# Load stage of a diagonal-LSTM and quantum-layer kernel: small loads on another queue, the first image in other pieces, early matmuls and an early table load

## The chip, the cores and the metric

The kernel runs on one core of one Trainium2 chip. A core has a matrix engine (TensorE, PE in the profile), a vector engine (DVE), a scalar engine for activations (ACT), a general one (POOL, GpSimd), a queue engine (SP), and 16 DMA engines that move data between device memory and the core's on-chip memory. Each engine works through its own list of instructions in order and waits on semaphores for the others. DMAs are issued from the lists of SP, ACT and POOL.

The metric is the device time of one execution in microseconds (us). Several executions are timed; the median counts.

## The reference

The input is `x` of shape 16 x 128 x 64 x 64 (images, channels, rows, columns), fp32. There are two layers, each with a residual sum. `gn` is a group normalisation with 32 groups of 4 channels.

```python
def lstm(x, w_is, b_is, w_ss, b_ss):          # x: [16, 128, 64, 64]
    xs = skew(x)                              # row i shifted right by i: 127 columns
    i_s = einsum('oi,bihw->bohw', w_is, xs) + b_is
    def step(carry, ist):                     # one column of the skewed image
        h, c = carry                          # [16, 128, 64 rows]
        h_shift = h moved down by one row
        gates = ist + w_ss[:, :, 0] @ h_shift + w_ss[:, :, 1] @ h + b_ss
        o, f, i = sigmoid(gates[:, :384]) in three parts
        g = tanh(gates[:, 384:])
        c = f * c + i * g
        h = o * tanh(c)
        return (h, c), h
    return unskew(scan(step, zeros, columns of i_s))

x = x + lstm(gn(x), w_is, b_is, w_ss, b_ss)
xq = tokens(gn(x)) @ pre_w.T + pre_b          # 4 angles for each pixel
z = simulate(xq, q_weights)                   # 4-qubit circuit, 2 layers of rotations and CNOTs
x = x + image(z @ post_w.T + post_b)
```

`q_weights` (2 x 4 x 3) are the angles of the rotations; the kernel turns them into sines and cosines once.

## The kernel before

Channels lie on the 128 partitions. Forty of an image's 64 rows stay in on-chip memory, in the tile `ring` (16 images x 40 rows x 64 columns for each channel); the other 24 rows are read for their statistics only, through one of two buffers (`rest`, `trio`), and read again later. The program has three stages: the load stage, the scan of 160 diagonal steps (two bands of 32 rows share the partitions' columns), and the output stage. All stages are written out by hand (`manual_schedule`): each engine runs its instructions in the order in which the program emits them.

The change lies in the load stage (the block `with ExitStack() as prep`). Two things go on there side by side.

*Images and statistics.* SP issues, image by image, `rows(b)` (L258 to L265: the 40 rows for `ring`) and `behind(b)` (L269 to L274: the other 24). DVE runs `statistics(b, k)` (L295) on the eight chunks of 8 rows of each image. Chunk `k` is counted by place in `ring`: chunk 0 holds rows 32 to 39, chunk 1 rows 0 to 7, chunk 2 rows 8 to 15, chunks 3 and 4 rows 16 to 31; chunks 5 to 7 are in `rest` or `trio`. A buffer is refilled when DVE has done its three chunks. The last four images end with `aggregated(b)` on DVE (L300); POOL does the others (`gathering`).

*Inverse steps.* Pixels that no image reaches yet have a zero input, so their state is the same for all; the kernel computes it once as 33 steps on one column (`inv_step`, L194). A step is four matmuls of 128 x 128 on PE (each fp32 matmul runs as two passes), four gate activations on ACT with one product on POOL between, then three more activations on ACT, the last of which writes `hinv` for the next step. From the fourth step on two matmuls without use (`keep`, L183) follow on PE. They write one PSUM buffer (`ps_keep`, one buffer), of which nothing is read.

Before the first step stand, on each engine in this order:

- ACT: six DMA issues (two halves of `w_ss` into `ws_n`, `q_weights` into `qw`, `b_is` and `b_ss` into `b_n`, `w_is` into `wx_n`), the sine of `turned()` (L351), the copy of `wsT` from PSUM (L369), the copy of the biases (L374), then the gates.
- POOL: the identity matrix `ident` (`make_identity`), six small DMA issues (L286 to L291), the memsets of `hinv` and `cinv`, `turned()` (L342 to L350, from `qw` to the argument of the sine), the sum of the biases (L375).
- DVE: two statistics of image 0, two sums of the two taps of `w_ss` (L405, one for each half), then statistics.
- PE: four transposes into `wsT_ps` with `ident` (L368), one of the biases (L373), then the step's matmuls (L203).

Between the first steps stand the list `between`: the transposes of `w_is` (`wxT`), of the two taps of `w_ss` (`w0T`, `w1T`), and so on. `qw`, `wx_n` and `ws_n` are parts of the tiles named `spare` in the profile.

After the last step POOL copies `hinv` into the first state (L469, L470), PE starts the first scan step's matmuls (L481), in the middle of which it takes the group means of the statistics (L491). From these come mean and inverse deviation of each image, the first normalised diagonal on POOL, and the scan.

ACT needs the right function table in place: a table load (`ACT_TABLE_LOAD`) stands ahead of the first activation of another set.

Of the kernel before, what the change touches and what calls it, by code (L numbers as in the profile page):

```python
# [11 lines left out]
F32 = mybir.dt.float32  # L12
AF = mybir.ActivationFunctionType
# [3 lines left out]
P = 128  # L17
# [3 lines left out]
SLOTS = 32  # L21
# [13 lines left out]
AHEAD = RING - SLOTS  # L35
# [47 lines left out]
def kernel(  # L83
# [16 lines left out]
    nc = tc.nc  # L100
# [38 lines left out]
    def place(r):  # L139

        return (r + AHEAD if r < SLOTS else r - SLOTS) * NW

    def block(r):

        return ring[:, :, place(r) : place(r) + BLOCK]
# [18 lines left out]
    with ExitStack() as scan:  # L164
# [4 lines left out]
        wsT = wpool.tile([P, 512], F32, name="wsT")  # L169
# [3 lines left out]
        cinv = wpool.tile([P, NH], F32, name="cinv")  # L173
# [6 lines left out]
        stats = spool.tile([P, NB, NG2, 6], F32, name="stats")  # L180
        ps_small = scan.enter_context(tc.tile_pool(name="ps_small", bufs=1, space=PSUM))

        def keep(pool, tag, v):  # L183

            ps = pool.tile([P, v.shape[-1]], F32, name=nc.get_next_instruction_name(), tag=tag)
            nc.tensor.matmul(ps, lhsT=wsT[:, 0:P], rhs=v, start=True, stop=True)

        def fill(n):

# [43 lines left out]
        with ExitStack() as prep:  # L233
            pp = prep.enter_context(tc.tile_pool(name="prep", bufs=1))
# [3 lines left out]
            ps_keep = prep_ps.enter_context(tc.tile_pool(name="ps_keep", bufs=1, space=PSUM))  # L238
            prep.enter_context(tc.manual_schedule())

            sum_n, wx_n = (v.rearrange("p (g c) -> p g c", g=4) for v in spare[4:6])
            ws_n = [v.rearrange("p (g c) -> p g c", g=2) for v in spare[6:8]]
            b_n = pp.tile([8, P], F32, name="b_n", tag="rows")
            four_sb, prew, preb = (spare[3][0:4, a:b] for a, b in ((0, 272), (272, 400), (400, 401)))
            post_n, qw = spare[3][:, 404:408], spare[3][:, 408:432]
            ident = pp.tile([P, P], F32, name="ident")
# [10 lines left out]
            rests = {}  # L257

            def rows(b):
                half = SLOTS // 2  # L260
                for r, n in ((0, half), (half, half), (SLOTS, AHEAD)) if b < 2 else ((0, SLOTS), (SLOTS, AHEAD)):
                    nc.sync.dma_start(
                        out=ring[:, b, place(r) : place(r) + n * NW],
                        in_=xv[b, :, r * NW : (r + n) * NW],
                    )  # L265
# [3 lines left out]
            def behind(b):  # L269
                rest = both_rests[b % 2]  # L270
                rests[b] = [rest[:, i] for i in range(3)]
                of = xv[b, :, RING * NW :].rearrange("p (k n) -> p k n", n=CHUNK)
                for k in ((0, 1), (1, 2), (2, 3)) if b in (0, NB - 1) else ((0, 3),):
                    nc.sync.dma_start(out=rest[:, slice(*k)], in_=of[:, slice(*k)])  # L274

            ws_v = w_ss.rearrange("(g o) c k -> o g (c k)", o=P)
            for i in range(2):
                nc.scalar.dma_start(out=ws_n[i], in_=ws_v[:, 2 * i : 2 * i + 2])
            nc.scalar.dma_start(
                out=qw, in_=q_weights.rearrange("l w a -> (l w a)").partition_broadcast(P)  # L280
            )
            nc.scalar.dma_start(out=b_n[0:4], in_=b_is.rearrange("(g o) -> g o", o=P))
            nc.scalar.dma_start(out=b_n[4:8], in_=b_ss.rearrange("(g o) -> g o", o=P))
            nc.scalar.dma_start(out=wx_n, in_=w_is.rearrange("(g o) c -> o g c", o=P))
            make_identity(nc, ident)
            nc.gpsimd.dma_start(out=wide_sb, in_=wide)  # L286
            nc.gpsimd.dma_start(out=four_sb, in_=four)
# [7 lines left out]
            def statistics(b, k):  # L295
                v = ring[:, b, k * CHUNK : (k + 1) * CHUNK] if k < 5 else rests[b][k - 5]
                nc.vector.bn_stats(stats[:, b, k, :], v)
# [43 lines left out]
            def turned():  # L341
                nc.gpsimd.tensor_add(ang[:, 1, 0, :], q3[:, 0, :], q3[:, 2, :])  # L342
                nc.gpsimd.tensor_sub(ang[:, 1, 1, :], q3[:, 0, :], q3[:, 2, :])
                nc.gpsimd.tensor_copy(ang[:, 1, 2, :], q3[:, 1, :])
                nc.gpsimd.tensor_scalar(
                    ang[:, 0], ang[:, 1], 1.0 / (4.0 * math.pi), 0.25, ALU.mult, ALU.add
                )
                nc.gpsimd.tensor_scalar_mul(ang[:, 1], ang[:, 1], 1.0 / (4.0 * math.pi))
                nc.gpsimd.tensor_scalar(rnd, ang, ROUND, ROUND, ALU.add, ALU.subtract)
                nc.gpsimd.tensor_sub(ang, ang, rnd)  # L350
                nc.scalar.activation(trig, ang, AF.Sin, scale=TWO_PI)  # L351
# [13 lines left out]
            def transposed(name, to, of):  # L365
                tp = ps_prep.tile([P, 512], F32, name=f"{name}_ps", tag="tp")
                for g in range(4):
                    nc.tensor.transpose(tp[:, g * 128 : (g + 1) * 128], of(g), ident)  # L368
                nc.scalar.copy(to, tp)  # L369

            def biases():
                tp = ps_prep.tile([P, 8], F32, name="bias_ps", tag="tp")
                nc.tensor.transpose(tp, b_n, ident[0:8, 0:8])  # L373
                nc.scalar.copy(bias8, tp)  # L374
                nc.gpsimd.tensor_add(bias, bias8[:, 0:4], bias8[:, 4:8])  # L375
# [12 lines left out]
            def output_weights():  # L388
# [6 lines left out]
                nc.scalar.copy(w_out, tp)  # L395

            rows(0)
            rows(1)
            behind(0)
            turned()  # L400
            for k in (1, 2):
                statistics(0, k)
            for i in range(2):
                v = ws_n[i]
                nc.vector.tensor_add(sum_n[:, 2 * i : 2 * i + 2], v[:, :, 0::2], v[:, :, 1::2])  # L405
            transposed("wsT", wsT, lambda g: sum_n[:, g, :])
            biases()

            def cleared():
                for v in (*hst, *xns, none, cst[:, :, 0:LEAST]):  # L410
                    nc.gpsimd.memset(v, 0.0)
                    yield
                nc.gpsimd.memset(eps, EPS)
                nc.gpsimd.tensor_sub(apart_of, ident, group)
                yield
                nc.gpsimd.memset(w_image, 0.0)
                yield
# [21 lines left out]
            for b in range(NB):  # L439
                while b < NB - 1 and done * (NB - 1) < EARLY * (b + 1):  # L440
                    inv_step(done, ps_inv)
                    some()
                    if done > 2:
                        for _ in range(2):
                            keep(ps_keep, "keep", wsT[:, 0:P])
                    if between:
                        between.pop(0)()
                    done += 1
                if b + 2 < NB:
                    rows(b + 2)  # L450
                if b + 1 < NB:
                    behind(b + 1)
                    for k in ORDERED:
                        statistics(b + 1, k)
                for k in (5, 6, 7):
                    statistics(b, k)
                if b >= 3 * GATHER:
                    aggregated(b)
                if b and b <= 3 * GATHER and b % GATHER == 0:
                    behind_pool.append(gathering(b - GATHER))  # L460
# [15 lines left out]
            ps = ps_small.tile([P, 2, NB], F32, name="gm1", tag="small")  # L476
            var = pp.tile([P, NB], F32, name="var1")
            for g in ORDER:
                first[g] = ps_gate.tile([P, 2, NC], F32, name=f"ps0_{g}", tag="gate")
                for w, rhs in ((w1T, hst[0][:, :, 0 : LEAST // 2]), (w0T, above(hst[0], 0, LEAST // 2))):  # L480
                    nc.tensor.matmul(  # L481
                        first[g][:, :, 0 : LEAST // 2],
                        lhsT=w[:, g * 128 : (g + 1) * 128],
                        rhs=rhs,
                        start=w is w1T,
                        stop=True,
# [8 lines left out]
            ps = ps_gate.tile([P, NB], F32, name="gv1", tag="gate")  # L495
# [167 lines left out]
        def gate_ps(t):  # L663

            a, b = wide(t, LEAST // 2)
            ps = {} if t else first
            for g in ORDER:
                if t:
                    ps[g] = ps_gate.tile([P, 2, NC], F32, name=f"ps{t}_{g}", tag="gate")
                nc.tensor.matmul(  # L670
                    ps[g][:, :, a:b],
                    lhsT=wxT[:, g * 128 : (g + 1) * 128],
                    rhs=xns[t % 2][:, :, a:b],
                    start=t > 0,
                    stop=True,
                    skip_group_check=True,
                )
            if twice(t):
                nc.tensor.matmul(
                    ps[GO][:, 1, a:b],  # L680
                    lhsT=wxT[:, GO * 128 : (GO + 1) * 128],
                    rhs=xns[t % 2][:, 0, a:b],
                    start=False,
                    stop=True,
                    skip_group_check=True,
                )
            return ps
# [275 lines left out]
        with tc.manual_schedule():  # L963
            normalised(0)
            normalised(1)
            ps = gate_ps(0)
            for t in range(NSTEP):
                ps = step(t, ps)
# [7 lines left out]
            warm = small.tile([P, 1], F32, name="warm", tag="inv_t")  # L976
            nc.scalar.activation(warm, shift, AF.Sqrt)
            ps = ps_small.tile([P, 2, NB], F32, name="gm3", tag="small")
# [11 lines left out]
            v = block(NH - ROWS).rearrange("p i (r w) -> p i r w", w=NW)[:, :, :, NW - STRIP :]  # L990
# [30 lines left out]
            ps = ps_small.tile([P, NB], F32, name="mr_ps", tag="small")  # L1021
# [221 lines left out]
```

## Time and profile before

| | us |
|---|---|
| median of 3 runs | 1403.12 (1402.34 to 1403.14) |
| the profiled execution | 1402.86 |
| its span | 1401.1 |
| PE busy | 1348.3 |
| DVE busy | 975.5 |
| POOL busy | 885.4 |
| ACT busy | 786.5 |

The span is the time from the first instruction to the last of the profiled execution; the rest of its time lies around it. Busy time is the union of an engine's instructions. The times of instructions below count from the start of the span.

The page divides the span into 40 slices of 35 us. Each digit is the busy share in tenths, the last row the rate of the DMA engines:

```
PE   6788999999999999999999999999999999989995
DVE  6973565577767776677776777766666566876996
DMA  9950000000000000133333100000000000004999
GB/s 359 418 210 1 2 1 1 1 1 1 1 1 1 0 1 1 61 121 121 120 121 120 61 1 1 1 1 1 1 1 1 1 0 1 2 30 145 388 402 357
```

The load stage is the first 95 us or so: the DMA engines are busy, DVE nearly so, PE less. Then comes the scan, in which PE is busy.

### The profile page before, as it was taken

To read this page: it belongs to the slowest core of one execution; us is meant where nothing else is said; L and a number is where in the kernel's file an instruction comes from. 1 tells how busy PE (TensorE), PEld (TensorE's weight loads), DVE (VectorE), ACT (ScalarE), POOL (GpSimd) and SP (SyncE) were. 2 spreads that over 40 slices of the span, in tenths; PEclk is the share of its full clock that TensorE was granted. 3 is DMA by queue.
4 is the path that set the end of the run, shared out by engine and by line. 5 is a ranking of instruction groups with operands and counts; after the bars stand their busy time and mean duration, and the time that the engine had idled before them with its cause. 6 is when DMAs were issued, how large, how long until landed. Compare 5 with 4: busy or idle time off the path is not lost.

```text
span 1401.1 us, 19953 instructions
## 1 busy us (share of the span) xinstructions
PE 1348.3 (96%) x6028; PEld 964.8 (69%) x6028; DVE 975.5 (70%) x2526; ACT 786.5 (56%) x1880; POOL 885.4 (63%) x1578
## 2 busy tenths in 40 slices
PE   6788999999999999999999999999999999989995
PEld 4668888777767777777777667776777778886332
DVE  6973565577767776677777776666665566876996
ACT  5765666555555555555555555555555566654331
POOL 3236777776666777777777766777777667653300
PEclk9999999999999999999999999999999999999998
DMA  9950000000000000133333100000000000004999
GB/s 359 418 210 1 2 1 1 1 1 1 1 1 1 0 1 1 61 121 121 120 121 120 61 1 1 1 1 1 1 1 1 1 0 1 2 30 145 388 402 357
DMA packets 58027, 107.03 MB, mean 76 GB/s; under 512 B 4368, under 2 KB 32048, under 8 KB 56128
## 3 DMA queue, kind: packets, MB, share of 16 engines
q1 hardware_dynamic: 53280, 94.39, 18.4%
q0 software_dynamic: 3408, 10.58, 2.1%
q8 instruction: 48, 0.79, 0.2%
q10 hardware_dynamic: 1232, 0.80, 0.2%
q14 instruction: 59, 0.48, 0.1%
HBM read 59.61 MB, written 46.14 MB: 75 GB/s over the span
## 4 chain that ended last, share of the span: by engine, by line
PE 84%; DVE 3%; ACT 1%; issue 1%; POOL 1%; DVEq 0%; ACTq 0%; POOLq 0%
PE ps L849 47%; PE ps L670 30%; PE po_None L1125 3%; PE theta_None L1074 2%; PE am_None L1103 1%; DVE spare L934 1%; DVE stats L798 0%; DVE ps L924 0%; PE po L1125 0%; DVE cst L927 0%; DVE ring L1143 0%; ACT g L868 0%; DVE ps L864 0%; ACT g L928 0%; ACT ps L868 0%
## 5 line engine op out<-in xcount | busy, mean ns | idle before, releaser
L670 PE MATMUL ps<-spare,wxT 128*128 128x512 f32 (+18 forms) x1280 | 479.7, 518 | 0.6 <-POOL spare L661 0.6
L864 DVE TENSOR_TENSOR ps<-ps,both 128x256 f32<-128x256 f32 (+9 forms) x536 | 219.7, 410 | 294.4 <-PE ps L849 291.2
L868 ACT ACTIVATE ps<-ps,bias 128x512 f32<-128x512 f32 (+23 forms) x480 | 279.5, 583 | 218.5 <-DVE ps L864 182.1
L670 PEld LDWEIGHTS ps<-spare,wxT 128*128 128x128 f32 x1280 | 231.0, 190 | 173.1 <-issue 155.4
L849 PE MATMUL ps<-trio,w1T 128*128 128x256 f32 (+14 forms) x1088 | 306.4, 363 | 0.0
L849 PE MATMUL ps<-trio,w0T 128*128 128x256 f32 (+14 forms) x1088 | 305.6, 362 | 0.0
L899 ACT COPY both<-ps 128x256 f32<-128x256 f32 (+9 forms) x536 | 189.6, 356 | 181.0 <-PE ps L849 161.4
L849 PEld LDWEIGHTS ps<-spare,wsT 128*128 128x128 f32 x1088 | 196.1, 190 | 78.3 <-DVE spare L934 30.6
L849 PE MATMUL ps<-spare,wsT 128*128 128x256 f32 (+14 forms) x1088 | 243.4, 365 | 1.8 <-DVE spare L934 1.6
L707 POOL TENSOR_TENSOR ring<-ring,spare 128x256 f32<-128x256 f32 (+15 forms) x375 | 231.5, 644 | 17.9 <-DVE spare L934 17.9
L849 PEld LDWEIGHTS ps<-trio,w1T 128*128 128x128 f32 x1088 | 201.7, 190 | 22.2
L849 PEld LDWEIGHTS ps<-trio,w0T 128*128 128x128 f32 x1088 | 201.2, 190 | 21.1
L661 POOL TENSOR_TENSOR spare<-spare,rstd 128x512 f32<-128x512 f32 (+10 forms) x160 | 170.9, 1068 | 14.2 <-DVE rstd L505 1.7
L655 POOL TENSOR_TENSOR spare<-ring 128x256 f32<-128x256 f32 (+13 forms) x165 | 139.4, 845 | 0.0
L928 ACT ACTIVATE g<-cst 128x256 f32<-128x256 f32 (+20 forms) x320 | 102.9, 368 | 63.7 <-DVE cst L927 63.3
L934 DVE TENSOR_TENSOR spare<-g,ps 128x256 f32<-128x256 f32 (+17 forms) x319 | 105.4, 368 | 44.4 <-ACT g L928 39.7
L697 POOL TENSOR_TENSOR trio<-spare 128x240 f32<-128x240 f32 (+9 forms) x136 | 102.7, 755 | 37.3 <-DVE spare L934 33.8
L649 POOL TENSOR_TENSOR spare<-ring,mean 128x256 f32<-128x256 f32 (+15 forms) x191 | 122.6, 642 | 2.5 <-DVE mean L494 2.0
L868 ACT ACTIVATE g<-ps,bias 128x512 f32<-128x512 f32 (+20 forms) x160 | 97.3, 608 | 27.8 <-DVE ps L864 21.9
L927 DVE TENSOR_TENSOR cst<-cst,ps 128x256 f32<-128x256 f32 (+20 forms) x320 | 104.5, 368 | 5.5
L924 DVE TENSOR_TENSOR ps<-ps,g 128x512 f32<-128x512 f32 (+20 forms) x160 | 94.9, 593 | 18.2 <-ACT g L868 18.1
L916 DVE TENSOR_TENSOR cst<-cst,ps 128x512 f32<-128x512 f32 (+20 forms) x160 | 92.7, 580 | 16.8 <-POOL spare L231 9.6
(379 smaller groups left out, 1161.7 us busy)
## 6 DMA issues: line engine op xcount, KB each, us to landing
out_dram<-ring SPq DMA_DIRECT2D x93, 256.0 KB, 4.9
ring<-in_x_dram SPq DMA_DIRECT2D x14, 1024.0 KB, 9.7
low<-ring SPq DMA_DIRECT2D x6, 2048.0 KB, 7.6
ring<-in_x_dram SPq DMA_DIRECT2D x6, 2048.0 KB, 8.2
trio<-in_x_dram SPq DMA_DIRECT2D x7, 768.0 KB, 7.6
rest<-in_x_dram SPq DMA_DIRECT2D x7, 768.0 KB, 7.9
ring<-low POOLq DMA_DIRECT2D x18, 256.0 KB, 6.8
ring<-in_x_dram SPq DMA_DIRECT2D x16, 256.0 KB, 9.9
```

The lines of the kernel that those rows point to most:

```text
L649: op = nc.gpsimd.tensor_sub(by_pairs(xn, 0, j0, j1), x0, over(mean1, j1 - j0))
L655: op = nc.gpsimd.tensor_sub(by_pairs(xn, 1, j0, j1), lower, of)
L661: nc.gpsimd.tensor_mul(v, v, r)
L670: nc.tensor.matmul(ps[g][:, :, a:b], lhsT=wxT[:, g * 128 : (g + 1) * 128], rhs=xns[t % 2][:, :, a:b], start=t > 0, stop=True, skip_group_c ...
L707: op = engine.tensor_add(x1, x1, by_pairs(new, q, j0, j1))
L849: nc.tensor.matmul(out, lhsT=w[:, g * 128 : (g + 1) * 128], rhs=rhs, start=False, stop=True, skip_group_check=True,)
L864: nc.vector.tensor_add(v, v, both[g][:, a:b])
L868: nc.scalar.activation(to[:, :, a:w], ps[g][:, :, a:w], FUNC[g], bias=bias[:, g : g + 1])
L899: nc.scalar.copy(both[g][:, a:b], ps[g][:, 0, a:b])
L927: nc.vector.tensor_add(c[:, q], c[:, q], ig[:, q])
L928: nc.scalar.activation(th[:, q, a:w], c[:, q], AF.Tanh)
L934: nc.vector.tensor_mul(new[:, q, a:v], th[:, q, a:v], act[GO][:, q, a:v])
```

## The change

In words:

- `q_weights`, `b_is` and `b_ss` are issued from POOL, ahead of `make_identity`, and no more from ACT.
- `w_is` is issued from SP, between the rows of image 0 and of image 1.
- Image 0's rows come as 8, 24 and 8 (before: 16, 16 and 8), and image 1's as 32 and 8 (before: 16, 16 and 8).
- `keep` takes its weights as an argument; twelve of them with `ident` as weights and as data stand ahead of the transposes of `wsT`.
- DVE's first instructions change order: statistic of chunk 1, sum of the first half of `w_ss`, statistic of chunk 2, sum of the second half.
- After the biases an activation of one column with Sigmoid is added, whose result is not used.

```diff
-        def keep(pool, tag, v):
+        def keep(pool, tag, v, w=wsT[:, 0:P]):
             ps = pool.tile([P, v.shape[-1]], F32, name=nc.get_next_instruction_name(), tag=tag)
-            nc.tensor.matmul(ps, lhsT=wsT[:, 0:P], rhs=v, start=True, stop=True)
+            nc.tensor.matmul(ps, lhsT=w, rhs=v, start=True, stop=True)
...
             def rows(b):
-                half = SLOTS // 2
-                for r, n in ((0, half), (half, half), (SLOTS, AHEAD)) if b < 2 else ((0, SLOTS), (SLOTS, AHEAD)):
+                for r, n in ((0, AHEAD), (AHEAD, SLOTS - AHEAD), (SLOTS, AHEAD))[b > 0 :]:
+                    if b and r < SLOTS:
+                        r, n = 0, SLOTS
                     nc.sync.dma_start(
...
             for i in range(2):
                 nc.scalar.dma_start(out=ws_n[i], in_=ws_v[:, 2 * i : 2 * i + 2])
-            nc.scalar.dma_start(
+            nc.gpsimd.dma_start(
                 out=qw, in_=q_weights.rearrange("l w a -> (l w a)").partition_broadcast(P)
             )
-            nc.scalar.dma_start(out=b_n[0:4], in_=b_is.rearrange("(g o) -> g o", o=P))
-            nc.scalar.dma_start(out=b_n[4:8], in_=b_ss.rearrange("(g o) -> g o", o=P))
-            nc.scalar.dma_start(out=wx_n, in_=w_is.rearrange("(g o) c -> o g c", o=P))
+            nc.gpsimd.dma_start(out=b_n[0:4], in_=b_is.rearrange("(g o) -> g o", o=P))
+            nc.gpsimd.dma_start(out=b_n[4:8], in_=b_ss.rearrange("(g o) -> g o", o=P))
             make_identity(nc, ident)
...
             rows(0)
+            nc.sync.dma_start(out=wx_n, in_=w_is.rearrange("(g o) c -> o g c", o=P))
             rows(1)
             behind(0)
+            for _ in range(12):
+                keep(ps_keep, "keep", ident, ident)
             turned()
-            for k in (1, 2):
-                statistics(0, k)
             for i in range(2):
                 v = ws_n[i]
+                statistics(0, 1 + i)
                 nc.vector.tensor_add(sum_n[:, 2 * i : 2 * i + 2], v[:, :, 0::2], v[:, :, 1::2])
             transposed("wsT", wsT, lambda g: sum_n[:, g, :])
             biases()
+            warm = pp.tile([P, 1], F32, name="warm1")
+            nc.scalar.activation(warm, cinv[:, 0:1], AF.Sigmoid)
```

## The prediction

> **What bounds the kernel now.** I read the page first (shares, chain of waits), then the timeline of the load stage's two ends, then SP's waits, then the windows of one microsecond.
>
> ```profile
> span 1401.1 us, 19953 instructions
> PE 84%; DVE 3%; ACT 1%; issue 1%; POOL 1%; DVEq 0%; ACTq 0%; POOLq 0%
> ```
>
> TensorE's scan holds the span; the change doesn't touch it. Whatever is won or lost must come from the time at which the scan can start. The timeline around that start (start, length, engine, line):
>
> ```profile
> 92.52 0.29 ACT L210 ACTIVATE hinv<-inv_t,inv_a 128x1 f32<-128x1 f32 x1
> 92.61 0.37 DVE L300 BATCH_NORM_AGGREGATE mv<-stats 128x2 f32<-128x48 f32 x1
> 93.00 0.18 POOL L470 COPY spare<-hinv 128x1 f32<-128x1 f32 x1
> 93.24 0.49 PE L481 MATMUL ps<-spare,w1T 128*128 128x128 f32 x2 [0.78 <-POOL spare L470]
> 94.23 0.29 PE L491 MATMUL gm<-mv,w_amp 128*128 128x16 f32 x2
> ```
>
> Two chains arrive almost together. The 33 inverse steps end with `hinv` at 92.81 and release POOL L470, then PE L481. The statistics end at 92.98 (L300); the mean's matmul L491 needs them, yet waits for L481's matmuls until 94.23. So the steps bound, and the statistics stand 94.23 - 93.08 = 1.15 us behind (0.1 us for the hand-over). How the steps begin:
>
> ```profile
> 8.68 0.20 POOL L342 TENSOR_TENSOR w_image<-spare 128x8 f32<-128x8 f32 x1 [3.73 <-DMA spare<-in_L_conv_q_weights_dram]
> 10.71 0.24 ACT L351 ACTIVATE w_image<-w_image 128x48 f32<-128x48 f32 x1 [5.50 <-POOL w_image L350]
> 10.86 0.57 ACT L369 COPY wsT<-wsT_ps 128x512 f32<-128x512 f32 x1
> 12.42 1.28 ACT L210 ACT_TABLE_LOAD   x1 [0.93 <-PE inv_ps L203]
> 13.72 0.72 ACT L210 ACTIVATE inv_a<-inv_ps,bias 128x1 f32<-128x1 f32 x4
> 15.38 2.07 PE L203 MATMUL inv_ps<-hinv,wsT 128*128 128x128 f32 x8 [0.91 <-ACT hinv L210]
> 21.90 1.16 PE L203 MATMUL inv_ps<-hinv,wsT 128*128 128x128 f32 x8 [0.62 <-ACT hinv L210]
> ```
>
> The transposes of `wsT` were done at 9.1, but their copy stood behind the Sin, which waits for `qw`. The same eight passes take 2.07 us at first and 1.16 from 21.90 on: `hinv` ends at 15.32, 18.58, 21.84, 24.18, so steps 1 and 2 take 3.26 us and later ones 2.34.
>
> **The change, part by part.** *Small loads to POOL.* `make_identity` now stands behind three issues. POOL's issues last 0.71 (`wide_sb`, 128 partitions) and 0.50 to 0.55 us, so `ident`, done at 1.29 before, is done at 1.29 + 0.71 + 2 x 0.54 = 3.1 (2.8 to 3.4, three of 0.50 or three of 0.71). [...]
>
> [...]
>
> *Twelve fillers.* They need only `ident` and stand on PE ahead of the transposes. A filler is L186's shape; each waits for the one before it, having one PSUM buffer:
>
> ```profile
> 22.89 0.38 PE L186 MATMUL I-294_295<-wsT 128*128 128x128 f32 x2
> 23.34 0.49 PE L186 MATMUL I-297_298<-wsT 128*128 128x128 f32 x2
> L203 PE MATMUL inv_ps<-hinv,wsT x24: 420/421/582, 11.6 to 20.3; 128*128 128x128 f32 x24
> ```
>
> The second one shows the price with its wait: 0.49 + 0.07 of gap = 0.56 us at full rate. At the early rate a pass takes 421 ns against 273, so a filler takes 0.56 + 2 x 0.15 = 0.86. When does the rate rise? PE worked 11.57 to 14.47, paused, then worked nearly unbroken from 15.38 to 20.6, where it rose; so 2.9 us weren't enough and 5.2 were. Fillers keep PE 0.79/0.86 = 92% busy from 3.1 on, so I put the rise at 6.0 to 8.3, middle 7.15. That is 4.7 fillers at 0.86 and 7.3 at 0.56: they end at 7.15 + 7.3 x 0.56 = 11.2 (10.8 to 11.7). That is later than `wsT`'s data (second half landed at 7.93, added by 8.4; all that is ahead of it now, 1.8 MB, is what had moved by 8 us before) and later than the Sin: the fillers set the start. Four transposes at full rate take 0.7 (half of 1.16, plus the tail), so the copy starts at 11.9 instead of 10.86.
>
> [...]
>
> *Sigmoid table.* Before, copy to first gate took 13.72 - 10.86 = 2.86, since the load waited 0.93 us for PE. Now it follows the bias copy (ended 0.64 after the copy's start): 0.64 + 1.28 + 0.16 = 2.1. PE's first gate, 0.7 + 0.4 after the copy, is hidden in it; without the early load it would be the 2.86 again. First gate: 11.9 + 2.1 = 14.0, so 0.3 us late.
>
> *Rate in the steps.* Steps 1 and 2 at 2.34 instead of 3.26 save 1.84; `wxT`'s copy (ends 15.79 in its place) still ends before the first gate of a step at full rate (15.38 + 0.53). Steps end 1.84 - 0.3 = 1.5 us earlier (1.0 to 1.9).
>
> *Rows and `w_is` on SP.* [...]
>
> ```profile
> SPq L262 <- DMA spare<-in_L_conv_w_ss_dram: 5.5, 2, 4.1
> 10.00:11.00 1.00, 0.00 (x0) 0.00 (x0) 0.48 (x1) 0.29 (x2) 0.60 (x2) 1.00 0.71 207
> 12.00:13.00 1.00, 1.00 (x7) 1.00 (x7) 1.00 (x2) 0.58 (x1) 0.00 (x0) 1.00 0.92 326
> 70.00:80.00 10.00, 8.10 (x56) 6.56 (x54) 9.85 (x18) 7.43 (x32) 1.32 (x7) 1.00 1.02 418
> ```
>
> [...] What is gained: the last column (GB/s) is 207 to 326 from 10 to 14 us against 418 later. By rate that is 1.35 us lost (0.58 more from 5 to 8), by engine share (0.71 to 0.92) only 0.6. The stream, and with it the last statistics, come 0 to 1.9 us earlier; I take 1.0, between the two readings. A loss is excluded: the bytes are the same, and `w_is` (needed by PE after step 0, near 14) is in front of image 1 with 0.6 us of them. DVE's statistic of chunk 2 now waits for 24 rows, and the second `w_ss` sum behind it, then PE; the fillers cover it up to 11. The other statistics wait too, but DVE idled over 5 us before 20.
>
> *Sum.* The gain is the smaller of the steps' 1.5 and the statistics' 1.15 + 1.0: 1.5. The profiled execution took 1402.86 (span 1401.1 and 1.76 around it), so 1401.4; the median of the runs, 1403.12, lies 0.26 above, so 1401.6. A difference within 0.2% (2.8 us) is about what a measurement of this kernel can't tell from no change.
>
> **The rivals.**
> *A, everything at its good end.* If a filler's wait is hidden, it costs two passes of 0.26 (2.07/8): 6.2 in all, ending at 9.3. The copy then starts at about 10.2 and the steps gain 1.4 + 1.84 = 3.2; the statistics cap it at 1.15 + 1.9 = 3.05: 1400.1. It passes 0.2% once the stream gains 1.65. For it: the low GB/s, the long SP stall. Against: each filler waits in the built order, and the engines were mostly busy in that stretch.
> *B, slower: the rate never rises under the fillers,* whose two passes leave gaps. They end at 3.1 + 12 x 0.86 = 13.4, transposes take 1.06 (the row of `wxT`), the copy starts at 14.5, the first gate at 16.6, 2.9 late; the fourth gate at the early rate adds 0.25, and steps 1 and 2 win nothing: 1406.2. It decides from fillers ending at 12.7 on (ten of them at 0.86), where the 1.84 is used up. For it: 2.9 us of work at 11.57 didn't raise the rate. Against: 92% busy.
> *C, the stream is hidden anyway.* It gains nothing, the statistics cap the gain at 1.15: 1402.0. For it: engine share near 1 all along.
>
> **How the numbers follow.** Forecast (1.0 to 1.9 gained) 0.32, C 0.10, A 0.33, B 0.25. Forecast and C lie within 0.2%: 0.42 for no change. A gives 0.33 for faster, B 0.25 for slower. The likeliest is 1401.6, its own range 1401.2 to 1402.1. The range goes from A's best part, 1399.6, to B less its last tenths, 1406.0.
>
> **What would show it.** In the profile after: twelve L186 pairs on PE from 3.1, with passes going from 421 to 273 ns between 6.0 and 8.3; `wsT`'s copy near 11.9, waiting for PE and not for the Sin; a table load right behind the bias copy; the first gate near 14.0; step 1 in 2.34; `hinv` of the last step near 91.3; L300 near 92; SP's first six issues before 4 us. Wrong: fillers ending before 10 or after 12.7, L491 waiting for DVE, or a scan that changes its pace.

## The result, and the profile after

| | before | after |
|---|---|---|
| median of 20 runs, us | 1402.64 (1401.41 to 1405.15) | 1405.33 (1404.37 to 1406.20) |
| ratio, 95% interval | | 1.0018 (1.0011 to 1.0024) |
| profiled execution, us | 1402.86 | 1406.04 |
| its span, us | 1401.1 | 1404.2 |

The changed kernel is slower, by 2.7 us. The lines of the program stand one to four further down than before (the scan's first matmul is L485, the mean's L495). The page's first line of the profile after, for the scale:

```profile
span 1404.2 us, 20004 instructions
```

The timeline of the load stage after (start, length, engine, line, tiles, and in brackets the idle time with what ended it):

```profile
3.28 0.29 POOL masks.py:199 TENSOR_SCALAR_AFFINE_SELECT ident<-ident 128x128 f32<-128x128 f32 x1
3.62 0.80 PE L186 MATMUL I-156_157<-ident 128*128 128x128 f32 x2 [3.62 <-POOL ident masks.py:199]
4.48 0.80 PE L186 MATMUL I-159_160<-ident 128*128 128x128 f32 x2
...
13.01 0.80 PE L186 MATMUL I-189_190<-ident 128*128 128x128 f32 x2
...
13.60 1.06 PE L368 MATMUL wsT_ps<-ident,spare 128*128 128x128 f32 x4
14.70 0.58 ACT L369 COPY wsT<-wsT_ps 128x512 f32<-128x512 f32 x1 [2.87 <-PE wsT_ps L368]
15.37 1.28 ACT L411 ACT_TABLE_LOAD   x1
16.77 0.57 ACT L210 ACTIVATE inv_a<-inv_ps,bias 128x1 f32<-128x1 f32 x3
18.66 2.07 PE L203 MATMUL inv_ps<-hinv,wsT 128*128 128x128 f32 x8 [0.33 <-ACT hinv L210]
21.92 1.16 PE L203 MATMUL inv_ps<-hinv,wsT 128*128 128x128 f32 x8 [0.42 <-ACT hinv L210]
```

Each filler pair takes 0.80 us and the next starts 0.854 us after it ((13.01 - 3.62) / 11), from the first to the last: the rate never rose under them. Only the pair of the step at 21.92 is at full rate (1.16 for eight passes); the clock record of the trace rises at 21.27, against 20.84 before. The copy of `wsT` had waited 2.87 us for PE: not `qw` and the Sin but the fillers set the start. So the first gate is at 16.77, 3.05 later than the 13.72 of before. The same view at the stage's end:

```profile
92.32 0.37 DVE L300 BATCH_NORM_AGGREGATE mv<-stats 128x2 f32<-128x48 f32 x1
...
95.07 0.29 ACT L210 ACTIVATE hinv<-inv_t,inv_a 128x1 f32<-128x1 f32 x1
...
95.78 0.49 PE L485 MATMUL ps<-spare,w1T 128*128 128x128 f32 x2 [0.78 <-POOL spare L474]
...
96.78 0.29 PE L495 MATMUL gm<-mv,w_amp 128*128 128x16 f32 x2
```

The steps end at 95.36 (92.82 before), the mean's matmul is at 96.78 (94.23), 2.55 later. The statistics end at 92.69, 0.29 earlier than before and 4 us ahead of the mean's matmul, so they don't bind. Behind the mean nothing changed: 3.00 us from L495 to the end of `rstd` in both. The 2.55 us make up nearly all of the 2.7 of the medians. From the end of `rstd` to the end of the span it is 1303.9 us before and 1304.5 after; over all the profiles below this stretch takes 1303.3 to 1305.3, so half a microsecond there tells nothing.

### The profile page after: what moved, and what is told of

Same layout as the page of the kernel before. It is cut to its first block, busy times and chain, and to the rows that moved or that the text cites. A ratio compares the mean times of both kernels' runs of the same rounds, so it can differ in the third digit from the quotient of the medians.

```text
span 1404.2 us, 20004 instructions
## 1 busy us (share of the span) xinstructions
PE 1356.4 (97%) x6052; PEld 969.7 (69%) x6052; DVE 975.7 (69%) x2526; ACT 786.5 (56%) x1881; POOL 887.0 (63%) x1581
## 5 line engine op out<-in xcount | busy, mean ns | idle before, releaser
L920 DVE TENSOR_TENSOR cst<-cst,ps 128x512 f32<-128x512 f32 (+20 forms) x160 | 92.7, 580 | 16.4 <-POOL spare L231 10.9
```

## The experiments

Times in the table are of the profiled executions, "gate" the first gate, "mean" the start of the mean's matmul (before: 10.86, 13.72, 92.98, 94.23, 97.23). The medians stand beside those of the kernel before on the same chip.

| kernel | median | before | ratio (95%) | copy | gate | statistics' end | mean | `rstd` |
|---|---|---|---|---|---|---|---|---|
| no fillers | 1402.48 | 1402.72 | 0.9999 (0.9991-1.0008) | 11.72 | 13.78 | 92.38 | 93.26 | 96.26 |
| packed, 12 | 1402.49 | 1402.72 | 0.9994 (0.9985-1.0004) | 11.87 | 13.92 | 92.49 | 94.51 | 97.51 |
| packed, 24 | 1402.58 | 1402.84 | 0.9996 (0.9988-1.0005) | 11.61 | 13.67 | 92.05 | 92.50 | 95.49 |
| weights first | 1402.31 | 1402.84 | 0.9996 (0.9987-1.0005) | 8.86 | 10.93 | 92.49 | 92.55 | 97.08 |
| the same, 19 packed | 1402.87 | 1402.76 | 0.9998 (0.9989-1.0006) | 8.70 | 10.77 | 91.73 | 91.78 | 96.32 |
| the same, 19 packed and ten held | 1400.81 | 1402.63 | 0.9983 (0.9974-0.9991) | 8.45 | 10.53 | 92.39 | 92.44 | 95.54 |

**No fillers.** The kernel after without

```diff
-            for _ in range(12):
-                keep(ps_keep, "keep", ident, ident)
```

> The changed kernel without its twelve early fillers, all else kept. Theory T (the fillers, each waiting for the one before, ran at the early rate to 13.8 us and held the transposes back): the copy of wsT is then set by the Sin, so it starts at about 11.8 instead of 14.7, the first gate at 13.9 instead of 16.8, the last hinv at about 93.0 instead of 95.4; median about 1402.8, that is 2.5 us less than the changed kernel and equal to the kernel before. Rival R (the moved loads are to blame: the second half of w_ss and the Sin come late): it stays within 0.7 us of the changed kernel, about 1405.

Without them the time is that of the kernel before (ratio 0.9999), so the fillers are the loss. What is left of the change comes to nothing in the medians: the copy of `wsT` waits for the Sin again and starts 0.86 later than before (the load of `q_weights` from POOL), and the early table gives 0.80 back. In the profiled execution the mean is still 0.97 earlier, since the rate rose at 16.61 there and not at 20.84 as in the profile before; the medians don't show it.

**Fillers alone,** on the kernel before:

```diff
+            for _ in range(12):
+                keep(ps_keep, "keep", ident, ident)
             turned()
```

> The kernel before with the twelve fillers added and nothing else. T: they start at about 1.6 us and end at 11.9, the transposes of wsT take 1.06, the copy starts at 13.0 instead of 10.9, the first gate at 15.8; the rate does not rise under them; median 1403.7 to 1404.8 (slower than before by 1.1 to 2.2 us). R: no change, 1402.7. My own forecast (the rate rises under fillers): L186 passes of 273 ns from 8 us on, fillers ending at 9.5, median 1401 to 1402.

1403.84, ratio 1.0009 (1.0000 to 1.0018), about 1.1 us slower and as T had it, though the interval reaches to no change. Here `ident` is ready at 1.3, and still the rate holds low from the first filler to the last (the timeline on PE):

```profile
1.35 0.80 PE L186 MATMUL I-157_158<-ident 128*128 128x128 f32 x2 [1.35 <-POOL ident masks.py:199]
2.21 0.80 PE L186 MATMUL I-160_161<-ident 128*128 128x128 f32 x2
...
10.74 0.80 PE L186 MATMUL I-190_191<-ident 128*128 128x128 f32 x2
```

Ten microseconds of pairs, and the last is as long as the first. The copy is 1.57 later than before (12.43), the first gate 1.58.

**Packed fillers.** The same twelve, into one tile, so that none waits for another:

```diff
-            for _ in range(12):
-                keep(ps_keep, "keep", ident, ident)
+            one = ps_keep.tile([P, P], F32, name="packed", tag="keep")
+            for _ in range(12):
+                nc.tensor.matmul(one, lhsT=ident, rhs=ident, start=True, stop=True, ...)
```

> The changed kernel, the twelve fillers writing one PSUM tile, so that none waits for another. T: 24 passes of 0.213 us from 3.6 to 8.8; the copy of wsT is set by the Sin at 11.8, the first gate at 13.9; if unbroken passes raise the rate (an idle stretch of 2 us follows), steps 1 and 2 take 2.34, the last hinv ends near 91.3 and the statistics (92.7) cap the gain: 1401.2; if not, 1402.8. R: about 1405.

This tells the theories apart: the rate rose at 7.09, 3.46 us after the first of them at 3.63. They ended at 8.21, out of the way. The rise was then lost again: PE stood mostly idle from 8.4 until the Sin, and the clock fell back to 0.50 at 13.92, when PE had taken up work again, as the windows of one microsecond show (the shares of PE, PEld, DVE, ACT and POOL, then the granted clock, the DMA share and GB/s):

```profile
9.00:10.00 1.00, 0.00 (x0) 0.00 (x0) 0.53 (x2) 0.00 (x0) 1.00 (x6) 1.00 1.21 430
14.00:15.00 1.00, 0.24 (x2) 0.00 (x0) 1.00 (x3) 0.97 (x7) 0.76 (x5) 0.50 1.07 404
18.00:19.00 1.00, 0.67 (x4) 0.27 (x3) 0.69 (x3) 0.94 (x4) 0.00 (x0) 0.50 1.06 430
```

(Before the first rise of a profile the clock's column reads 1.00, since no change is on record yet; there the rate is read from the length of a pass, 421 ns before the rise and 273 after it in the kernel before.)

**`q_weights` on ACT.** No fillers, and the load issued from ACT behind `w_ss` as in the kernel before:

```diff
-            nc.gpsimd.dma_start(
+            nc.scalar.dma_start(
                 out=qw, in_=q_weights.rearrange("l w a -> (l w a)").partition_broadcast(P)
             )
```

> The changed kernel without fillers and with q_weights issued from ACT again (behind w_ss). If POOL's broadcast of q_weights holds the DMA engines up (89 GB/s in 6 to 7 us of the changed kernel): no such hole, chunk 2's rows land near 7 instead of 8.8, the second half of w_ss near 8 instead of 10.1, the Sin starts near 10.7 and the copy at 10.9, the first gate at 13.0 thanks to the early table load: 1402.0, 0.8 less than the run without fillers alone. If the hole comes from the sum of early issues instead, it stays and the time is that of the run without fillers, 1402.8.

1403.09, ratio 1.0003 (0.9994 to 1.0012). The first branch of the expectation failed: the start came later and not earlier. The second is not contradicted, as neither this run nor the one without fillers can be told from the kernel before. `qw` landed 9.2 us after its issue instead of 7.1, so the copy started at 13.23 instead of 11.72, and the hole in the DMA rate was not POOL's: it moved with the load. The windows without fillers, first from POOL, then from ACT (last column GB/s):

```profile
6.00:7.00 1.00, 0.27 (x2) 0.00 (x0) 0.00 (x0) 0.00 (x0) 0.16 (x1) 1.00 1.33 62
7.00:8.00 1.00, 0.00 (x0) 0.00 (x0) 0.00 (x0) 0.00 (x0) 0.00 (x0) 1.00 0.52 182
8.00:9.00 1.00, 0.00 (x0) 0.00 (x0) 0.44 (x1) 0.00 (x0) 0.34 (x1) 1.00 1.07 380
```

```profile
6.00:7.00 1.00, 0.38 (x2) 0.00 (x0) 0.00 (x0) 0.00 (x0) 0.38 (x3) 1.00 1.04 388
8.00:9.00 1.00, 0.00 (x0) 0.00 (x0) 0.10 (x2) 0.00 (x0) 0.00 (x0) 1.00 0.64 140
```

**Weights first.** No fillers; `q_weights` as ACT's first load, one half of `w_ss` behind it and the other as SP's first, biases on ACT, both sums ahead of the statistics:

```diff
-            for i in range(2):
-                nc.scalar.dma_start(out=ws_n[i], in_=ws_v[:, 2 * i : 2 * i + 2])
-            nc.gpsimd.dma_start(
+            nc.scalar.dma_start(
                 out=qw, in_=q_weights.rearrange("l w a -> (l w a)").partition_broadcast(P)
             )
+            for i, queue in enumerate((nc.scalar, nc.sync)):
+                queue.dma_start(out=ws_n[i], in_=ws_v[:, 2 * i : 2 * i + 2])
...
-                statistics(0, 1 + i)
...
+            for k in (1, 2):
+                statistics(0, k)
```

> The changed kernel without fillers, with the weights in front: q_weights first on ACT's queue, then the first half of w_ss and the biases; the second half of w_ss first on SP's; both sums on DVE ahead of its statistics; nothing small on POOL in front of the identity. T2 (the small loads' late landing set the start once the fillers are gone): q_weights lands near 5.5 instead of 8.9, the Sin starts near 8, the copy of wsT near 8.2, the first gate near 10.3, the last hinv ends near 89.3. Two chains bound the stage, so the statistics (92.4 to 93.0 in all runs so far) then set the mean's matmul, near 92.8 instead of 94.2: median 1401.2. If the steps alone bound the stage, the whole 3.5 us show: 1399.2. If q_weights' small pieces hold the DMA engines up from any queue, the hole in GB/s moves to 4 to 6 us and the statistics end later than 93.

`qw` lands 4.2 us after its issue, the Sin is at 7.04, the first gate at 10.93, and the steps end at 88.38, 4.44 earlier than before. The time is unchanged. The timeline around the mean says why:

```profile
92.12 0.37 DVE L300 BATCH_NORM_AGGREGATE mv<-stats 128x2 f32<-128x48 f32 x1
92.55 0.61 PE L494 MATMUL gm<-mv,w_amp 128*128 128x16 f32 x2 [2.59 <-DVE mv L300]
93.42 0.77 PE L484 MATMUL ps<-spare,w1T 128*128 128x128 f32 x2
```

PE now waits 2.59 us for the statistics, which are where they were. That caps the gain at 1.7. And while PE idled its clock fell to 0.50 (at 91.25, 1.3 us into the idle stretch): the pair L484 takes 0.77 us instead of 0.49, and from the mean to `rstd` it is 4.5 us instead of 3.0, which gives the rest back.

The other executions agree with the profiled one. The granted clock, as a mean over the whole execution, is on record for every one, and 6.8 us at 0.50, as from 91.25 here, would take 0.0024 off it (an estimate, 6.83 x 0.5 / 1401). It is 0.992 to 0.994 in all eleven executions of this kernel, and 0.995 or 0.996 in 82 of 106 of the kernel before. Those 82 have a median of 1402.5 us; the other 24, at 0.992 to 0.994, of 1404.1. The mean doesn't tell where in an execution the clock was low, but it seems that the kernel before, too, loses its clock now and then, and that this is part of its scatter.

**Ten fillers** instead of twelve, one execution:

```diff
-            for _ in range(12):
+            for _ in range(10):
```

> The changed kernel with ten fillers instead of twelve. T: each takes 0.855 us in line, so they end at 12.1 instead of 13.8 and the copy of wsT starts at 13.0 instead of 14.7. If the copy hung on anything else in that stretch it would not move by 1.7.

The copy moved from 14.70 to 12.99, by 1.71, two times 0.854: each serial filler lies on the path in full. The mean moved by more, 2.60 (96.78 to 94.18): here the rate rose at 17.05 and not at 21.27, so one step less was done at the early rate (step 1 in 2.38 instead of 3.26). The time was 1402.61, but of a single execution.

**24 packed fillers,** the edit of the twelve with the larger number, to bridge PE's idle time:

> The changed kernel with 24 fillers into one PSUM tile (48 passes). [...] If the rate falls again before the steps, as with twelve, the last hinv ends near 93: 1402.5.

The load stage did as the forecast of the prediction had wanted. On the timeline:

```profile
3.63 7.40 PE L403 MATMUL packed<-ident 128*128 128x128 f32 x48 [3.63 <-POOL ident masks.py:199]
...
11.61 0.57 ACT L369 COPY wsT<-wsT_ps 128x512 f32<-128x512 f32 x1
...
13.67 0.70 ACT L210 ACTIVATE inv_a<-inv_ps,bias 128x1 f32<-128x1 f32 x4
...
15.31 0.94 PE L203 MATMUL inv_ps<-hinv,wsT 128*128 128x128 f32 x6 [1.42 <-ACT hinv L210]
```

The rate rose at 7.38 and held; steps 1 and 2 took 2.34. In the profiled execution `rstd` ends 1.74 earlier than before, but the span, 1400.2, is only 0.9 shorter: 0.8 is lost behind `rstd`, where the profiles differ by up to 2 us anyway. It is also the second fastest of its ten executions (1401.92); their median is 1402.58, and the interval holds 1. A fall of the clock isn't the reason, since its mean is 0.995 or 0.996 in all ten. A later rise may be: in the latest of the profiles with packed fillers it came 4.99 us after the first filler, here 3.75. By the pass times of this profile (0.213 us before the rise, 0.112 after it) that would end the fillers 0.6 us later, an estimate, and as the steps bind here it would show in full. That was not tried; why the median gains so little stays open.

**Table alone,** on the kernel before:

```diff
             biases()
+            warm = pp.tile([P, 1], F32, name="warm1")
+            nc.scalar.activation(warm, cinv[:, 0:1], AF.Sigmoid)
```

> The kernel before with the early sigmoid alone. My term: copy to first gate 2.1 instead of 2.86, so the first gate at 13.0, everything up to the last hinv 0.76 earlier (92.05), the mean's matmul at 93.47: median 1401.9, 0.05% less. If the table load is hidden anyway: no change in the first gate, 13.7.

Copy to first gate 2.05 (11.00 to 13.05) against 2.86, as costed. The median doesn't show it: 1402.95, ratio 1.0002 (0.9990 to 1.0014). Its profiled execution (1409.81, the slowest of its twelve) tells nothing of the end of the stage, since there the loads ran slower (380 GB/s from 60 to 80 us, 418 before) and the statistics ended at 98.9.

**Rows and `w_is` on SP alone,** on the kernel before: the pieces of images 0 and 1 of the change, and

```diff
-            nc.scalar.dma_start(out=wx_n, in_=w_is.rearrange("(g o) c -> o g c", o=P))
...
             rows(0)
+            nc.sync.dma_start(out=wx_n, in_=w_is.rearrange("(g o) c -> o g c", o=P))
             rows(1)
```

> The kernel before with the new row pieces of images 0 and 1 and w_is on SP, nothing else changed; ACT keeps its five other issues. Prediction's reading (the stream gains, a loss is excluded): SP's stall shortens, the last aggregate ends 0.3 to 1.9 us earlier than 92.98, but the steps still bound; first gate near 13.7 to 14.2, last hinv within 0.9 us of 92.8; time within 0.1% of before, at or below 1402.6. Rival (chunk 2 now waits for 24 rows and the second sum of w_ss with it): chunk 2's statistic and what stands behind it on DVE come later; since here both statistics stand ahead of both sums, the sums end after 9.5 and the copy of wsT waits for PE and not for the Sin, first gate after 14.2.

1402.92 against 1402.63, ratio 0.9998 (0.9990 to 1.0006): no difference. The statistics ended at 92.76, 0.22 earlier, below the 0.3 I expected. The first gate came at 14.28, past the point named for the rival, but not by its mechanism: the sums ended at 9.36, and the copy waited for the Sin, whose `qw` had landed about half a microsecond later. The small loads on POOL and DVE's new order were not tried each by itself.

**Held clock.** From the weights-first kernel, two theories joined: packed fillers at the start, and ten packed matmuls ahead of the mean so that PE doesn't idle there.

```diff
+            one = ps_keep.tile([P, P], F32, name="packed", tag="keep")
+            for _ in range(19):
+                nc.tensor.matmul(one, lhsT=ident, rhs=ident, start=True, stop=True, ...)
             turned()
...
                 if g == GI:
+                    held = ps_gate.tile([P, P], F32, name="held", tag="gate")
+                    for _ in range(10):
+                        nc.tensor.matmul(held, lhsT=wxT[:, 0:P], rhs=w0T[:, 0:P], ...)
```

(The two `keep` behind the mean write one tile here, so that no more buffers are used.)

> The weights-first order without serialised fillers, plus 19 packed fillers (one PSUM tile, no waits) from about 1.4, ten packed matmuls ahead of the mean's matmul, and the two matmuls behind it in one tile. Theory (the clock needs unbroken passes and falls when PE idles): the rate rises about 3.5 us after the first filler, at 4.9 to 8.3; the copy of wsT is at 8.2 to 9.5, first gate at 10.3 to 11.6, steps 1 and 2 in 2.34, last hinv at 85.5 to 88.5. The statistics stay where they are (last aggregate 92 to 93) and set the mean's matmul at 92.5 or so; PE's ten matmuls shorten its idle time ahead of it, so the rate holds or falls for less, and the inverse deviation stands 3.0 us behind the mean: 95.5 to 96, 1.2 to 1.7 earlier than before. Time then 1401.0 to 1401.7 with the kernel before at 1402.6. Rival 1 (the rate falls anyway, as in the weights-first run, since PE idles from about 87 to 89): inverse deviation at 97, no gain, 1402.3 or more. Rival 2 (PE's early work slows the loads or DVE): the last aggregate ends after 93.5.

1400.81 against 1402.63, ratio 0.9983 (0.9974 to 0.9991): the only kernel here that is faster than the kernel before. The rate rose at 4.48 and stayed. PE's timeline ahead of the mean:

```profile
89.15 2.40 PE L498 MATMUL held<-w0T,wxT 128*128 128x128 f32 x20
...
92.44 0.40 PE L500 MATMUL gm<-mv,w_amp 128*128 128x16 f32 x2 [0.89 <-DVE mv L300]
```

Of the idle time 0.89 us is left, and `rstd` ends 3.10 behind the mean, at 95.54: 1.69 earlier than before. The medians differ by 1.82.

**The same without the ten,** beside a second run of the kernel with them, unchanged.

> The kernel that was faster (weights first, 19 packed fillers, ten packed matmuls ahead of the mean's matmul), without those ten matmuls. Theory (the ten keep PE from idling before the scan, so that the rate doesn't fall): the first gate and the last hinv stay at about 10.5 and 87.7, the statistics at 92.4; PE then idles from 89.0 to 92.4, and the rate falls there in this run as it did in the weights-first run (4.5 us from the mean's matmul to the inverse deviation instead of 3.0 to 3.1), so the time is 1402.0 to 1402.6. Rival (the ten do nothing, the early rate alone brings the gain): 3.0 to 3.1 us from mean to inverse deviation, time at 1400.8 to 1401.2 as with them.

> The faster kernel again, unchanged, beside the one without its ten matmuls on the same chip. Expected: 1400.5 to 1401.2, ratio to before 0.997 to 0.9995. If it was chance or that chip, about 1402.5.

Without the ten 1402.87, ratio 0.9998 (0.9989 to 1.0006); with them 1400.94, 0.9985 (0.9976 to 0.9994), against 1402.76. The steps end at the same time (88.00 and 87.69). The windows from 90 to 94, first without, then with the ten in the held kernel's first run:

```profile
90.00:92.00 2.00, 0.22 (x1) 0.22 (x2) 1.70 (x4) 0.00 (x0) 0.00 (x0) 0.92 0.00 0
92.00:94.00 2.00, 2.00 (x10) 2.00 (x11) 0.26 (x2) 0.18 (x1) 0.23 (x1) 0.50 0.00 0
```

```profile
90.00:92.00 2.00, 1.55 (x14) 1.35 (x13) 1.98 (x4) 0.00 (x0) 0.00 (x0) 1.00 0.00 0
92.00:94.00 2.00, 1.56 (x14) 1.56 (x15) 0.64 (x3) 0.18 (x1) 0.23 (x1) 1.00 0.00 0
```

Without the ten the clock falls to 0.50 at 91.68, 2.1 us into an idle stretch of 2.2; with them it stays at 1.00. In the second window ten passes keep PE busy throughout without the ten matmuls, and with them fourteen leave a fifth of it free. From the mean to `rstd` it is 4.54 against 3.10 us. The mean clock says the same of every execution: 0.993 or 0.994 in all eleven without the ten, 0.995 or 0.996 in all 23 with them. That difference is shown to be the clock, and the ten matmuls to be what holds it. Whether the 19 early fillers have a part in the gain was not tried: the weights-first kernel has none, and its steps, too, end 4 us ahead of the statistics.

## Why the prediction was wrong

The forecast was 1401.6; 1405.33 lies inside the range and next to rival B. By the prediction's steps:

1. *`ident` at 3.1:* 3.57. POOL's first issue started at 1.25, where before POOL's work on `ident` started at 0.72. Half a microsecond, all on the path here, since fillers follow.
2. *A filler at the early rate takes 0.86:* 0.854, and each lies on the path in full (ten fillers).
3. *"Fillers keep PE 0.79/0.86 = 92% busy from 3.1 on, so I put the rise at 6.0 to 8.3":* this is the step that failed. The share in which a pass is under way did not tell when the clock rises. In two kernels such pairs, under way for 0.80 of every 0.854 us, ran 10.2 us (3.62 to 13.81 after, 1.35 to 11.54 with the fillers alone) without a rise. With the packed ones it rose 3.1 to 5.0 us after the first (3.46 with twelve, 3.75 with 24, 3.12 and 4.99 with 19). In the twelve packed fillers, ahead of the rise, the view of their line reads (count, shortest, median and longest pass in ns, first and last start)

```profile
L403 PE MATMUL packed<-ident x15: 421/421/580, 3.6 to 6.8; 128*128 128x128 f32 x15
```

Behind the first, a pass starts every 0.213 us and lasts 0.421. So the next one starts halfway through it, and by that spacing, as an estimate, the two of a serial pair make up half of its 0.854 (2 x 0.213). The prediction took their whole length for work. Only these two densities were tried, 4.7 and 2.3 starts a microsecond (1 / 0.213 and 2 / 0.854), so what the clock does between them stays open. The rival's own argument ("whose two passes leave gaps") was the right one, and it stood at 0.25.
4. *Fillers end at 11.2, copy at 11.9, first gate at 14.0:* 13.81, 14.70, 16.77. Rival B had 13.4, 14.5 and 16.6, so its price held: it is 0.4 us short, and the late `ident` is 0.47; its time, 1406.2, lies 0.9 above the median.
5. *Steps 1 and 2 save 1.84:* step 1 took 3.26 and step 2 2.34 (before: 3.26 both). The rate rose at 21.27, nearly when it did before, and by then one step less had been done, so one step less was done at the early rate. B, whose fillers never raised the rate, had nothing saved here: 0.92 was. The first gate was 3.05 late, the fourth gate at the early rate added 0.24 (B: 0.25), less 0.92 makes 2.37; the last step was 2.54 late, and 0.17 came along the way.
6. *Small loads to POOL, the fillers' end at 11.2 later than the Sin:* no run shows the Sin ending by 11.2 with the loads on POOL. It ended at 11.82, before the fillers' 13.81 but later than the 10.95 of before. The load of `qw` took 7.3 us from POOL, where in the kernel before POOL's small loads had taken 5.0 to 5.8 and `qw` itself 6.8 from ACT, and `b_out`, queued ahead of the arithmetic, waited 2.72 us for it. This is hidden under the fillers, but it is what makes the change neutral without them. Measured are 7.1 to 7.3 us from POOL, and from ACT 9.2 behind `w_ss` without fillers, 6.8 in the kernel before and 4.2 as its first load. So in these runs what was ahead of the load and beside it decided more than the engine.
7. *Sigmoid table, copy to gate 2.1:* 2.07. Right.
8. *The statistics come 1.0 earlier; a loss is excluded:* 0.29 earlier, and 0.22 with the rows and `w_is` alone. That the stream gains because SP no longer waits was the author's estimate, and no run shows the 1.0: SP's first six issues did go out by 4.1 us, but behind them SP waited 5.2 us for `w_ss` (5.5 before). The low rate from 10 to 14 us is gone (415 GB/s from 10 to 11, 207 before). It was given back from 6 to 8, where the windows after read

```profile
6.00:7.00 1.00, 0.92 (x3) 0.50 (x2) 0.00 (x0) 0.00 (x0) 0.15 (x1) 1.00 1.15 89
7.00:8.00 1.00, 0.90 (x3) 0.61 (x3) 0.00 (x0) 0.00 (x0) 0.00 (x0) 1.00 0.51 169
```

against 338 and 282 before. Chunk 2's statistic waited 3.28 us in it, and the second sum of `w_ss` came at 10.12 instead of 7.93. Rival C, that the stream is hidden, was right as to the statistics: they ended between 91.7 and 93.4 in all profiles but that of the table alone, whatever the order of the loads. What sets that end was not isolated.
9. *The scan's chain:* the prediction took the smaller of two gains, and took 1 us earlier at the mean as 1 us of time. The weights-first kernels show a third limit that it had not seen: when the statistics bound and PE idled for 2.59 and 2.21 us, its clock fell to 0.50, and the time from the mean to `rstd` grew by 1.5 (4.5 against 3.0). Whether rival A's gain would have met the same limit was not tried.

Idle gaps of PE ahead of the mean of 2.59 us (weights first) and 2.21 us (19 packed, without the ten) cost the clock, which fell to 0.50 1.3 and 2.1 us into them; one of 0.89 us (with the ten) did not.

## What to carry to other kernels

Give dummy matmuls for warm-up one PSUM tile: those that waited for each other didn't raise the clock here in 10.2 us, those in one tile did in 3.1 to 5.0. Look at how many passes a microsecond start (2.3 against 4.7 here), not at how busy the engine looks (0.80 of 0.854 us). Before pricing an earlier start, see what binds next at the join, and what the engine that then waits loses by waiting: here the gain appeared only when ten matmuls without use kept TensorE busy for 2.4 us of that wait.

## What was not expected of the hardware

- The broadcast of `q_weights` to 128 partitions (12 KB) goes with a hole in the DMA rate. In four kernels that issue it from POOL the microsecond from 6 to 7 has 37 (twelve packed), 62 (no fillers), 88 (24 packed) and 89 GB/s (after), behind 348 to 410 in the one before; from ACT behind `w_ss` the one from 8 to 9 has 140, behind 336. It moves with the load: as ACT's first load this one was issued at 0.72 and landed 4.2 us later, and from 3 to 5 us the rate was 142 and 261 GB/s, where the kernel without fillers has 281 and 433. That the broadcast makes the hole was not tried by leaving it out.
- Without packed fillers the rate rose anywhere between 12.7 and 21.3 us in the profiles (12.7 with the weights first, where the first gate was at 10.9, 16.61 without fillers, 17.05 with ten, 20.84 before, 21.27 after), and each step that it comes later costs 0.92 us (3.26 against 2.34). Gains below a microsecond in this stage drown in it. Part of that seems to be chance: the two kernels with 19 packed fillers are the same up to the mean, and the rate rose 3.12 us after the first filler in one (with the ten) and 4.99 in the other. Once up, it stayed up for 1368.74 us both before and after (from 20.84 and from 21.27), and for 6.83 with twelve packed fillers (7.09 to 13.92). What sets the time of a rise was not shown. That serial fillers saw none in 10.2 us was the same in both kernels with twelve of them, whose rates rose at 21.27 and 20.36.
